# Ordering by hand what a graph kernel does before its first gather

## The chip, the cores and the metric

The program runs on one core of one Trainium2 chip. The metric is the device time of one execution in microseconds (us). A core has five engines with a queue each: TensorE (PE in the profile), VectorE (DVE), ScalarE (ACT), GpSimd (POOL) and SyncE (SP). DMAs are issued from the queues of SP, ACT and POOL.

## What is computed

There are N = 4096 nodes with 128 features in x and a 0/1 matrix adj of 4096 x 4096, in which each row has about 32 ones. Two layers follow one another, both over the neighbours that adj lists:

```
# layer 0, graph attention with 8 heads
Wh  = einsum('nd,hde->hne', x, W)
f1  = einsum('hnd,hd->hn', Wh, a1);  f2 = einsum('hnd,hd->hn', Wh, a2)
e   = leaky_relu(f1[:, :, None] + f2[:, None, :], 0.2)
att = softmax(where(adj > 0, e, -9e15), axis=-1)
h   = elu(einsum('hnm,hmd->hnd', att, Wh))
x1  = layernorm(x + elu(concat_heads(h) @ W1 + b1)) * gamma + beta
# layer 1, quantiles over the neighbours
keep = neighbours, less every m-th one (m = ceil(n/2) where n > 5, else 1)
agg  = mean of the 0.25, 0.5 and 0.75 quantiles of x1 over keep
out  = (0.5*agg + 0.5*x1) @ Wl.T + bl + x1
```

## The kernel before

Since a row has few neighbours, the kernel doesn't multiply by adj. It finds the list of each node's neighbours, sorts the nodes of a block by their number of neighbours, and gathers rows of x from DRAM by list. The 32 tiles of 128 nodes are worked on in three blocks of 4, 9 and 19 tiles (BLOCKS).

**The search** (`neighbours`) turns a tile of adj into lists. ACT takes the sign of half a tile (L568, `sgn`, two buffers). PE makes 512 keys at a time in PSUM (two buffers), each from two matmuls: L607 with `markb` marks a neighbour, and L610 adds its place, from the table `parts` (64 x 4096, zeros but for rows 0 and 32). DVE takes the eight largest keys of each 128 columns (L574, four MAX8), and picks the tile's 64 largest in eight rounds of MAX8 and MATCH_REPLACE8 (L579, L581) into `rec[:, t, 0:64]`, while the keys of the next tile are made. The search is a Python generator. It yields once for each 512 keys; I call that a piece. For the first block of four tiles there are 43 pieces, numbered from 0: 32 with keys, eight in which only the last tile's rounds of picking are left, and three for `complete_records`, which counts, takes out the removed neighbours and writes the lists as integers. Loads of adj (1 MB each, three buffers) go out on ACT's queue, the next one after each sign (L561).

**The rows** (`node_rows`) bring x into `rec`, multiply W by a1 and a2 on DVE (L507, L510) into `wa`, a 128 x 16 matrix, and then for each of the 32 tiles: PE transposes x (L514), ACT copies that to `xT` (L516), PE multiplies it by `wa` (L518), ACT copies the result to `F` (L519); two buffers for each. DVE clamps F into `rec` (L521) and derives a bound check from it (L523 to L528). Four DMAs write rows of 136 numbers (x and f2) to `xt_d` in DRAM, which is what the attention gathers.

**After that**, `rank_by_count` gives each node its place in the block by number of neighbours (DVE and PE; its last operation is L750, `ranks`). POOL scatters the four tiles of `rec` to DRAM by rank (L187), SP reads them back as `R` (L786), DVE makes lists and attention terms of them (L787 to L820, `f1b` and `f1x`), and POOL starts to gather (L178, `G<-xt_d,idx`). From here on POOL gathers to the end: rows of x for the attention (1180 gathers), then rows of x1 for the quantiles (1024).

**What sets the order.** Two parts of the kernel are a `manual_schedule` over DVE, PE, ACT and POOL: in them each of these engines issues its instructions in the order in which the program emits them. These are the attention with the searches of blocks 1 and 2 (from L382), and the sort at the end. Everything ahead of them, so the search of block 0 and the rows, is left to the framework's scheduler, which picks the next instruction for each engine itself. SP's order is always the scheduler's. Where a hand-ordered part's instructions fall among others of the same engine is the scheduler's too. An engine carries out its queue in order.

The tables `own` and `ownT` (L240 to L257) hold, for each width of list, which rows belong to which node; the attention reads them. `before` is a triangular mask for the ranks.

Of the kernel before, what the change touches and what calls it, by code (L numbers as in the profile page):

```python
# [9 lines left out]
F32 = mybir.dt.float32  # L10
BF16 = mybir.dt.bfloat16
I32 = mybir.dt.int32
AF = mybir.ActivationFunctionType
ALU = mybir.AluOpType
# [5 lines left out]
P = 128  # L20
N = 4096
# [180 lines left out]
def kernel(  # L202
# [30 lines left out]
    eps_t = const.tile([P, 1], F32, name="eps_t")  # L233
    nc.vector.memset(eps_t, EPS)
    pidx = const.tile([P, 1], F32, name="pidx")
    iota(nc, pidx, [[0, 1]], cm=1)
    jp1 = const.tile([P, L], F32, name="jp1")
    iota(nc, jp1, [[1, L]], base=1)

    own = {}  # L240
    for w in (32, 16, 8, 4):
        k = P // w
        v = const.tile([P, k], F32, name=f"v{w}")
        iota(nc, v, [[-w, k]], cm=1)
        own[w] = const.tile([P, k], F32, name=f"own{w}")
        nc.vector.tensor_scalar(own[w], v, 0.0, None, ALU.is_ge)
        nc.vector.scalar_tensor_tensor(own[w], v, float(w), own[w], ALU.is_lt, ALU.mult)


    ownT = {}  # L250
    for w in (32, 16, 8, 4):
        k = P // w // 4
        v = const.tile([4, k, P], F32, name=f"vT{w}")
        iota(nc, v, [[-4 * w, k], [1, P]], cm=-w)
        ownT[w] = const.tile([4, k, P], F32, name=f"ownT{w}")
        nc.vector.tensor_scalar(ownT[w], v, 0.0, None, ALU.is_ge)
        nc.vector.scalar_tensor_tensor(ownT[w], v, float(w), ownT[w], ALU.is_lt, ALU.mult)  # L257

    vecs = const.tile([P, 4, D], F32, name="vecs")
    W_sb = const.tile([P, H, D], F32, name="W_sb")  # L260
    W1_sb = const.tile([P, H, D], F32, name="W1_sb")
    nc.sync.dma_start(W_sb, W.rearrange("h d e -> d h e"))
    wa = const.tile([P, 2 * H], F32, name="wa")
    WlT = const.tile([P, D], F32, name="WlT")
    total = const.tile([1, 1], I32, name="total")
    bad = const.tile([P, 5, NT], F32, name="bad")
    consts = dict(
        W_sb=W_sb, W1_sb=W1_sb, vecs=vecs, eps_t=eps_t, ident=ident, own=own, ownT=ownT
    )
    own_i = const.tile([P, NT], I32, name="own_i")  # L270


# [5 lines left out]
    adjp = tc.alloc_tile_pool(name="adjp", bufs=2, side="right")  # L278
    cp = tc.alloc_tile_pool(name="cnt", bufs=2, side="right")
    kp = tc.alloc_tile_pool(name="key_ps", bufs=2, space=PSUM)  # L280
    nc.gpsimd.iota(
        rec.bitcast(I32)[:, :, R_OWN], pattern=[[P, NT]], base=0, channel_multiplier=1
    )
    parts = adjp.tile([64, N], BF16, name="parts", bufs=1)
    markb = adjp.tile([P, P], BF16, name="markb", bufs=1)
    nc.vector.memset(oneb, 1.0)
    nc.vector.tensor_scalar(markb, ident, MARK, None, ALU.mult)

    nc.gpsimd.memset(parts, 0.0)
    iota(nc, parts[0:1, :], [[-64, N // 64], [0, 64]], base=N)  # L290
    iota(nc, parts[32:33, :], [[0, N // 64], [-1, 64]])
    rowi = adjp.tile([P, P], F32, name="rowi", bufs=1)
    iota(nc, rowi, [[1, P]])
    nc.vector.tensor_scalar(before, rowi, pidx, None, ALU.is_gt)

    def search(t0, n):
        return neighbours(
            tc, adjp, cp, kp, rec, num, adj, t0, n, parts, markb, oneb, bad, jp1, pidx
        )

    for _ in search(0, BLOCKS[0]):
        pass
    with tc.tile_pool(name="setup", bufs=1) as sp, tc.tile_pool(
        name="setup_ps", bufs=2, space=PSUM
    ) as pp:
        node_rows(tc, sp, pp, rec, x, W_sb, a1, a2, Wl, wa, WlT, ident, bad, xt_d)
        nc.sync.dma_start(W1_sb, W1.rearrange("(h e) o -> e h o", e=P))
        for i, v in enumerate((b1, gamma, beta, bl)):
            nc.sync.dma_start(vecs[:, i, :], v.partition_broadcast(P))
        for i, big in enumerate((-BIG, BIG)):  # L310
            fill = sp.tile([P, D], F32, name=f"fill{i}")
            nc.vector.memset(fill, big)
            nc.sync.dma_start(x1_d[N + i * P : N + (i + 1) * P, :], fill)
    attp = tc.alloc_tile_pool(name="att", bufs=2, reuse_waits="tile")
    pp = tc.alloc_tile_pool(name="att_ps", bufs=1, space=PSUM)
# [2 lines left out]


    weigh, store, tail = [], [], []  # L320
    consts["small"] = pp.tile([P, 512], F32, name="small")

    narrow = {
# [58 lines left out]
    with tc.manual_schedule(engines=ORDERED):  # L382
        ranks = rank_by_count(tc, cp, kp, num, jp1, before, oneb, 0, BLOCKS[0])
        for v in store_records(0, 0, ranks):
            scatter(nc, *v)
        for b, n in enumerate(BLOCKS):
            last = b == len(BLOCKS) - 1
            if last:
                cp.release()
                adjp.release()  # L390
                keep = tc.alloc_tile_pool(name="keep", bufs=1, side="right")
                wt = keep.tile([P, NT, L], F32, name="wt")
                idx = keep.tile([P, NT, L], I32, name="idx")
                cp = tc.alloc_tile_pool(name="cnt_all", bufs=2, side="right", reuse_waits="tile")
                pieces, left = None, 0
            else:
                pieces, left = search(t0 + n, BLOCKS[b + 1]), pieces_of(BLOCKS[b + 1])
            ready.append(prepare(b, 0, t0))
            for i in range(n):
                among = []  # L400
                if last and 2 < i < n - 5:
                    among = [
                        (all_d, rec[:, t, 0:REC1], ranks[:, t : t + 1])
                        for t in range((i - 3) * NT // (n - 8), (i - 2) * NT // (n - 8))
                    ]
                if not last and i == n - 1:

                    for _ in pieces:
                        pass
                    left = 0  # L410
# [12 lines left out]
                if last and i == n - 5:  # L423
                    R = cp.tile([P, NT, REC1], F32, name="R", bufs=1)
                    nc.sync.dma_start(R, all_d.rearrange("(t p) w -> p t w", p=P))
                    pieces = lists_of_layer_1(
                        tc, cp, kp, R, jp1, pidx, ones, idx, own_i, bad, total, wt
                    )
                    left = -(-LIST_PIECES // 4)
            for _ in pieces or ():  # L430
                pass
            t0 += n
        for _ in range(5):
            step()
        check_bounds(tc, cp, kp, ones, bad, total)
# [49 lines left out]
        general_quantiles(tc, adj, x1_d, x1T_d, out, ident, WlT, vecs[:, 3, :])  # L485


def node_rows(tc, sp, pp, rec, x, W_sb, a1, a2, Wl, wa, WlT, ident, bad, xt_d):

    nc = tc.nc  # L490
    c = NT // 4
    for i in range(4):
        nc.sync.dma_start(
            rec[:, ts(i, c), R_X : R_X + D],
            x[ts(i, c * P), :].rearrange("(t p) d -> p t d", p=P),
        )
    a_b = sp.tile([P, 2, H * D], F32, name="a_b")
    for i, a in enumerate((a1, a2)):
        nc.sync.dma_start(a_b[:, i, :], a.rearrange("h d -> (h d)").partition_broadcast(P))
    wl_sb = sp.tile([P, D], F32, name="wl_sb")  # L500
    nc.scalar.dma_start(wl_sb, Wl)
    wl_ps = pp.tile([P, D], F32, name="xt_ps")
    nc.tensor.transpose(wl_ps, wl_sb, ident)
    nc.scalar.copy(WlT, wl_ps)
    for i in range(2):
        wprod = sp.tile([P, H, D], F32, name="wprod")
        nc.vector.tensor_tensor(  # L507
            wprod, W_sb, a_b[:, i, :].rearrange("p (h d) -> p h d", h=H), ALU.mult
        )
        nc.vector.tensor_reduce(wa[:, ts(i, H)], wprod, AX.X, ALU.add)  # L510
    F = sp.tile([P, NT, 2 * H], F32, name="F")
    for t in range(NT):
        xt_ps = pp.tile([P, P], F32, name="xt_ps")
# [3 lines left out]
        f_ps = pp.tile([P, 2 * H], F32, name="f_ps")  # L517
        nc.tensor.matmul(f_ps, lhsT=xT, rhs=wa, start=True, stop=True)  # L518
        nc.scalar.copy(F[:, t, :], f_ps)  # L519
    for dst, src in ((R_F1, F[:, :, 0:H]), (R_X + D, F[:, :, H:])):  # L520
        nc.vector.tensor_scalar(rec[:, :, dst : dst + H], src, FMAX, -FMAX, ALU.min, ALU.max)  # L521
    sq = sp.tile([P, NT, 2 * H], F32, name="sq")
    nc.vector.tensor_tensor(sq, F, F, ALU.mult)  # L523
    fm = sp.tile([P, NT], F32, name="fm")
# [1 line left out]

    nc.vector.tensor_scalar(fm, fm, FMAX * FMAX, None, ALU.is_le)
    nc.vector.tensor_scalar(bad[:, 3, :], fm, -1.0, 1.0, ALU.mult, ALU.add)  # L528
    for i in range(4):
        nc.sync.dma_start(  # L530
            xt_d[ts(i, c * P), :].rearrange("(t p) w -> p t w", p=P),
            rec[:, ts(i, c), R_X:],
        )
    pad = sp.tile([P, XW], F32, name="pad")
    nc.vector.memset(pad[:, 0:D], 0.0)
    nc.vector.memset(pad[:, D:], PADF)
    nc.sync.dma_start(xt_d[N:, :], pad)


def groups_of(n):  # L540
# [850 lines left out]
```

## Time and profile before

| | us |
|---|---|
| median of three runs | 3857.79 |
| lowest, highest | 3854.88, 3884.28 |
| profiled execution | 3857.37 |
| its span in the trace | 3855.5 |

| engine | busy us in the span | instructions |
|---|---|---|
| POOL | 2807.9 | 2388 |
| DVE | 2671.4 | 6439 |
| PE | 1253.7 | 5433 |
| ACT | 403.4 | 603 |

The stage that the change touches ends with the first gather at 113.86 us. The rest is attention to some 1884 us and quantiles to the end.

How to read the profile: times count from the start of the span. A line of the timeline has its start, its length, engine, line of the program, operation, output<-input, shapes and count; in brackets stands how long the engine had been idle before it and what it waited for ("<-PE key L610": the matmul that wrote key). A line of the waits has who waited, for whom, the sum, how often, and the longest. PEld is PE's load of weights. "issue" is time for which the trace shows no wait. SPq and ACTq are DMA issues in those engines' queues.

### The profile page before, as it was taken

What the parts mean: (1) busy time and instruction counts of PE and PEld (TensorE: products, weight loads), DVE (VectorE), ACT (ScalarE), POOL (GpSimd) and SP (SyncE); (2) the same over time, 40 slices, a digit from 0 to 9 for tenths busy, and PEclk for the clock granted to TensorE, in tenths of its full rate; (3) what the DMA queues carried; (4) which work ended last, traced back from release to release, by engine and by line L of the source; (5) the groups of instructions that cost most, each with busy time, mean ns of one, the idle gap of its engine ahead of it and who ended that gap; (6) DMA issues with size and microseconds to landing.
All of it is one profiled execution on the core that took longest, in us unless ns stands there. A gap on an engine that the chain in (4) does not pass through costs nothing. (4 is left out here: it accounts for less than half of the span.)

```text
span 3855.5 us, 21960 instructions
## 1 busy us (share of the span) xinstructions
PE 1253.7 (33%) x5433; PEld 961.2 (25%) x5433; DVE 2671.4 (69%) x6439; ACT 403.4 (10%) x603; POOL 2807.9 (73%) x2388
## 2 busy tenths in 40 slices
PE   6483867863746444455600000000000000000001
PEld 2143534543635444444500000000000000000000
DVE  8774688782522222257436888669999999998788
ACT  3111223210111101111100000000000000000000
POOL 1657674577777777777478888877788887888882
PEclk9975666655665555555555555555555555555555
DMA  6423444322222222222111111111111111111110
GB/s 213 153 88 106 150 139 132 122 54 65 54 55 53 54 53 54 64 58 55 34 47 38 41 39 34 38 42 41 41 38 28 32 35 44 38 35 38 38 40 16
DMA packets 110281, 241.25 MB, mean 63 GB/s; under 512 B 46976, under 2 KB 63360, under 8 KB 101952
## 3 DMA queue, kind: packets, MB, share of 16 engines
q0 software_dynamic: 76160, 160.24, 15.3%
q10 hardware_dynamic: 9360, 67.18, 5.1%
q1 hardware_dynamic: 24624, 12.34, 1.3%
q8 instruction: 45, 0.74, 0.1%
q14 instruction: 92, 0.75, 0.1%
HBM read 228.44 MB, written 11.15 MB: 62 GB/s over the span
## 5 line engine op out<-in xcount | busy, mean ns | idle before, releaser
L178 POOL DMA_INDIRECT vals<-x_d,idx x1024 | 1415.6, 1382 | 314.4 <-issue 303.8
L178 POOL DMA_INDIRECT G<-xt_d,idx x1180 | 1173.6, 995 | 483.4 <-issue 339.9
L1117 DVE TENSOR_TENSOR work<-work 128x256 f32<-128x256 f32 (+7 forms) x1168 | 921.5, 823 | 0.7
L1137 PE MATMUL st_ps<-dg,goal 128*128 128x128 f32 x286 | 71.9, 429 | 1791.9 <-DVE goal L1117 1704.4
L1117 DVE TENSOR_TENSOR work<-work,work 128x512 f32<-128x512 f32 (+4 forms) x820 | 584.3, 738 | 1.3
L1137 PEld LDWEIGHTS st_ps<-dg,goal 128*128 128x128 f32 x286 | 63.7, 324 | 1798.4 <-issue 1797.5
L926 PE MATMUL y<-wide,G 128*128 128x32 f32 (+3 forms) x2360 | 480.1, 382 | 21.9 <-DVE wide L914 21.9
L926 PEld LDWEIGHTS y<-wide,G 128*128 128x128 f32 x2360 | 460.0, 297 | 45.8 <-DVE wide L914 24.2
L869 DVE TENSOR_TENSOR z<-G,f1x 128x128 f32<-128x128 f32 (+2 forms) x92 | 29.9, 335 | 471.6 <-DMA G<-xt_d,idx 468.5
L1117 DVE TENSOR_TENSOR work<-vals 128x768 f32<-128x768 f32 (+11 forms) x64 | 128.8, 2028 | 267.8 <-DMA vals<-x_d,idx 265.7
L574 DVE MAX8 first<-key 128x8 f32<-128x128 f32 x1024 | 227.5, 282 | 112.5 <-PE key L610 112.5
L607 PE MATMUL key<-sgn,markb 128*128 128x512 bf16 x256 | 142.0, 555 | 160.9 <-DVE first L574 107.5
L883 PE MATMUL small<-z,own 128*4 128x32 f32 (+3 forms) x436 | 50.4, 284 | 368.1 <-ACT z L876 368.1
L1136 ACT ACTIVATE dg<-ident,wt 128x128 f32<-128x128 f32 x143 | 47.5, 394 | 1105.0 <-PE st_ps L1137 1104.6
L568 ACT ACTIVATE sgn<-adj_t 128x2048 bf16<-128x2048 int32 x64 | 122.1, 1907 | 343.0 <-PE key L607 328.2
L898 PE MATMUL rz<-rden,ownT 4*128 4x32 f32 (+3 forms) x436 | 107.1, 419 | 117.9 <-DVE rden L894 96.5
L610 PE MATMUL key<-parts,oneb 64*128 64x512 bf16 x256 | 140.6, 550 | 6.3 <-POOL parts L196 6.3
L956 PE MATMUL small<-W_sb,late 128*128 128x128 f32 x512 | 118.9, 426 | 33.6 <-DVE late L953 33.6
L898 PEld LDWEIGHTS rz<-rden,ownT 4*128 4x128 f32 x436 | 94.5, 310 | 134.0 <-DVE rden L894 68.3
L187 POOL DMA_INDIRECT out_dram<-o,own_i x32 | 67.9, 2123 | 79.9 <-ACT o L1163 56.2
L883 PEld LDWEIGHTS small<-z,own 128*4 128x4 f32 x436 | 27.1, 102 | 385.8 <-ACT z L876 373.3
L956 PEld LDWEIGHTS small<-W_sb,late 128*128 128x128 f32 x512 | 110.2, 327 | 44.9 <-DVE late L953 43.9
(179 smaller groups left out, 1879.3 us busy)
## 6 DMA issues: line engine op xcount, KB each, us to landing
adj_t<-in_adj_dram ACTq DMA_DIRECT2D x64, 1024.0 KB
G<-xt_d,idx POOLq DMA_INDIRECT x1180
vals<-x_d,idx POOLq DMA_INDIRECT x1024
R<-rec_d SPq DMA_DIRECT2D x128, 26.2 KB
xt_d<-rec SPq DMA_DIRECT2D x4, 544.0 KB
rec<-in_x_dram SPq DMA_DIRECT2D x4, 512.0 KB
W_sb<-in_L_gnn_W_dram SPq DMA_DIRECT2D x2, 512.0 KB
a_b<-in_L_gnn_a_dram SPq DMA_DIRECT2D x2, 512.0 KB
```

The costliest lines, as they stand in the source:

```text
L178: nc.gpsimd.indirect_dma_start(out=dst, out_offset=None, in_=rows, in_offset=bass.IndirectOffsetOnAxis(ap=idx, axis=0),)
L187: return nc.gpsimd.indirect_dma_start(out=rows, out_offset=bass.IndirectOffsetOnAxis(ap=idx, axis=0), in_=src, in_offset=None,)
L568: nc.scalar.activation(sgn, adj_t, AF.Sign, accum_out=cnt[:, i : i + 1])
L574: nc.vector.max(first[:, ts(c0 // CW + c, 8)], key[:, ts(c, CW)])
L607: nc.tensor.matmul(key, lhsT=markb, rhs=sgn[:, ts(b, 512)], start=True, stop=False)
L610: nc.tensor.matmul(key, lhsT=oneb[0:64, :], rhs=parts[:, ts(r, 512)], start=False, stop=True)
L883: nc.tensor.matmul(den[0:4, :].rearrange("p (g r h) -> p r g h", r=k // 4, h=H)[:, r], lhsT=own[w][:, ts(r, 4)], rhs=z[:, layer[i] : layer ...
L898: nc.tensor.matmul(rz[:, layer[i] * H : (layer[i] + w) * H], lhsT=ownT[w][:, r, :], rhs=rden.rearrange("p (g r h) -> p r g h", r=k // 4, h ...
L926: nc.tensor.matmul(yf[:, ts(g, c)], lhsT=G[:, col + g - g0, 0:D], rhs=pf[:, ts(g, c)], start=(i == 0 and g % (w // 2) == w // 2 - 1), stop ...
L956: nc.tensor.matmul(o, lhsT=hv[:, h, :], rhs=consts["W1_sb"][:, h, :], start=(h == 0), stop=(h == H - 1))
L1117: nc.vector.tensor_tensor(slots_of(dst, (j, c, s, m), size), slots_of(a, (i, c, s, m), size), slots_of(b, (i + d, c, s, m), size), op,)
L1137: nc.tensor.matmul(st_ps[:, u, :], lhsT=goal[:, (j * k + u) * D : (j * k + u + 1) * D], rhs=dg, start=(j == 0), stop=False,)
```

## The change

The part ahead of the attention becomes a third hand-ordered region, and its steps are emitted in another order:

- The tables for the keys come first: `parts` (cleared by DVE, no longer by POOL), `oneb`, the two iotas of `parts`, `markb`, and then `pidx`, `jp1`, the own numbers and `rowi`. `before` is made behind the search.
- `node_rows` becomes a generator too. After each piece of the search from piece 1 on, it advances by one step. Step by step: load W; load a1, a2, Wl; then x in four loads, three pieces apart; the two products of W; two tiles of x in each of 16 steps; clamps, the writes to `xt_d` and the padding row; the bound check; Wl's transpose.
- The loads of W, a1, a2 and x are issued from ACT instead of SP.
- `own` and `ownT` are made in the attention's region, behind the ranks and scatters of block 0.
- The padding row and two fill tiles are cleared by POOL, no longer by DVE.

```diff
-    own = {}
-    for w in (32, 16, 8, 4):
...
-    nc.sync.dma_start(W_sb, W.rearrange("h d e -> d h e"))
...
-    nc.gpsimd.memset(parts, 0.0)
...
-    for _ in search(0, BLOCKS[0]):
-        pass
     with tc.tile_pool(name="setup", bufs=1) as sp, tc.tile_pool(
         name="setup_ps", bufs=2, space=PSUM
-    ) as pp:
-        node_rows(tc, sp, pp, rec, x, W_sb, a1, a2, Wl, wa, WlT, ident, bad, xt_d)
+    ) as pp, tc.manual_schedule(engines=ORDERED):
+
+        nc.vector.memset(parts, 0.0)
+        nc.vector.memset(oneb, 1.0)
+        iota(nc, parts[0:1, :], [[-64, N // 64], [0, 64]], base=N)
+        iota(nc, parts[32:33, :], [[0, N // 64], [-1, 64]])
+        nc.vector.tensor_scalar(markb, ident, MARK, None, ALU.mult)
+        iota(nc, pidx, [[0, 1]], cm=1)
+        iota(nc, jp1, [[1, L]], base=1)
+        nc.gpsimd.iota(
+            rec.bitcast(I32)[:, :, R_OWN], pattern=[[P, NT]], base=0, channel_multiplier=1
+        )
+        iota(nc, rowi, [[1, P]])
+        rows = node_rows(tc, sp, pp, rec, x, W, W_sb, a1, a2, Wl, wa, WlT, ident, bad, xt_d)
+        for i, _ in enumerate(search(0, BLOCKS[0])):
+            if i > 0:
+                next(rows, None)
+        for _ in rows:
+            pass
+        nc.vector.tensor_scalar(before, rowi, pidx, None, ALU.is_gt)
         nc.sync.dma_start(W1_sb, W1.rearrange("(h e) o -> e h o", e=P))
...
-            nc.vector.memset(fill, big)
+            nc.gpsimd.memset(fill, big)
...
         for v in store_records(0, 0, ranks):
             scatter(nc, *v)
+
+        own = {}
+        for w in (32, 16, 8, 4):
+            k = P // w
+            v = const.tile([P, k], F32, name=f"v{w}")
+            iota(nc, v, [[-w, k]], cm=1)
...
+        ownT = {}
...
@@ node_rows
     nc = tc.nc
     c = NT // 4
+    load = nc.scalar.dma_start
+    load(W_sb, W.rearrange("h d e -> d h e"))
+    yield
+    a_b = sp.tile([P, 2, H * D], F32, name="a_b")
+    for i, a in enumerate((a1, a2)):
+        load(a_b[:, i, :], a.rearrange("h d -> (h d)").partition_broadcast(P))
+    wl_sb = sp.tile([P, D], F32, name="wl_sb")
+    load(wl_sb, Wl)
+    yield
     for i in range(4):
-        nc.sync.dma_start(
+        for _ in range(3):
+            yield
+        load(
             rec[:, ts(i, c), R_X : R_X + D],
             x[ts(i, c * P), :].rearrange("(t p) d -> p t d", p=P),
         )
...
-    wl_ps = pp.tile([P, D], F32, name="xt_ps")
-    nc.tensor.transpose(wl_ps, wl_sb, ident)
-    nc.scalar.copy(WlT, wl_ps)
     for i in range(2):
         wprod = sp.tile([P, H, D], F32, name="wprod")
...
         nc.vector.tensor_reduce(wa[:, ts(i, H)], wprod, AX.X, ALU.add)
+        yield
     F = sp.tile([P, NT, 2 * H], F32, name="F")
     for t in range(NT):
         xt_ps = pp.tile([P, P], F32, name="xt_ps")
         nc.tensor.transpose(xt_ps, rec[:, t, R_X : R_X + D], ident)
         xT = sp.tile([P, P], F32, name="xT", bufs=2)
         nc.scalar.copy(xT, xt_ps)
         f_ps = pp.tile([P, 2 * H], F32, name="f_ps")
         nc.tensor.matmul(f_ps, lhsT=xT, rhs=wa, start=True, stop=True)
         nc.scalar.copy(F[:, t, :], f_ps)
+        if t % 2:
+            yield
     for dst, src in ((R_F1, F[:, :, 0:H]), (R_X + D, F[:, :, H:])):
         nc.vector.tensor_scalar(rec[:, :, dst : dst + H], src, FMAX, -FMAX, ALU.min, ALU.max)
+    for i in range(4):
+        nc.sync.dma_start(
+            xt_d[ts(i, c * P), :].rearrange("(t p) w -> p t w", p=P),
+            rec[:, ts(i, c), R_X:],
+        )
+    pad = sp.tile([P, XW], F32, name="pad")
+    nc.gpsimd.memset(pad[:, 0:D], 0.0)
+    nc.gpsimd.memset(pad[:, D:], PADF)
+    nc.sync.dma_start(xt_d[N:, :], pad)
+    yield
...
+    yield
+    wl_ps = pp.tile([P, D], F32, name="xt_ps")
+    nc.tensor.transpose(wl_ps, wl_sb, ident)
+    nc.scalar.copy(WlT, wl_ps)
```

More of the change, by code (lines that the diff above doesn't have):

```diff
@@ L235 @@
     pidx = const.tile([P, 1], F32, name="pidx")
-    iota(nc, pidx, [[0, 1]], cm=1)
     jp1 = const.tile([P, L], F32, name="jp1")
-    iota(nc, jp1, [[1, L]], base=1)
-    own = {}
-    for w in (32, 16, 8, 4):
[L242 to L257, printed above, removed]
     vecs = const.tile([P, 4, D], F32, name="vecs")
@@ L266 @@
     bad = const.tile([P, 5, NT], F32, name="bad")
-    consts = dict(
-        W_sb=W_sb, W1_sb=W1_sb, vecs=vecs, eps_t=eps_t, ident=ident, own=own, ownT=ownT
-    )
     own_i = const.tile([P, NT], I32, name="own_i")
@@ L280 @@
     kp = tc.alloc_tile_pool(name="key_ps", bufs=2, space=PSUM)
-    nc.gpsimd.iota(
-        rec.bitcast(I32)[:, :, R_OWN], pattern=[[P, NT]], base=0, channel_multiplier=1
-    )
     parts = adjp.tile([64, N], BF16, name="parts", bufs=1)
     markb = adjp.tile([P, P], BF16, name="markb", bufs=1)
-    nc.vector.memset(oneb, 1.0)
-    nc.vector.tensor_scalar(markb, ident, MARK, None, ALU.mult)
-    nc.gpsimd.memset(parts, 0.0)
-    iota(nc, parts[0:1, :], [[-64, N // 64], [0, 64]], base=N)
-    iota(nc, parts[32:33, :], [[0, N // 64], [-1, 64]])
     rowi = adjp.tile([P, P], F32, name="rowi", bufs=1)
-    iota(nc, rowi, [[1, P]])
-    nc.vector.tensor_scalar(before, rowi, pidx, None, ALU.is_gt)
     def search(t0, n):
@@ L320 @@
     weigh, store, tail = [], [], []
+    consts = {}
     consts["small"] = pp.tile([P, 512], F32, name="small")
@@ L385 @@
             scatter(nc, *v)
+        own = {}
[3 more added lines that the diff above has]
+            iota(nc, v, [[-w, k]], cm=1)
+            own[w] = const.tile([P, k], F32, name=f"own{w}")
+            nc.vector.tensor_scalar(own[w], v, 0.0, None, ALU.is_ge)
+            nc.vector.scalar_tensor_tensor(own[w], v, float(w), own[w], ALU.is_lt, ALU.mult)
+        ownT = {}
+        for w in (32, 16, 8, 4):
+            k = P // w // 4
+            v = const.tile([4, k, P], F32, name=f"vT{w}")
+            iota(nc, v, [[-4 * w, k], [1, P]], cm=-w)
+            ownT[w] = const.tile([4, k, P], F32, name=f"ownT{w}")
+            nc.vector.tensor_scalar(ownT[w], v, 0.0, None, ALU.is_ge)
+            nc.vector.scalar_tensor_tensor(ownT[w], v, float(w), ownT[w], ALU.is_lt, ALU.mult)
+        consts.update(
+            W_sb=W_sb, W1_sb=W1_sb, vecs=vecs, eps_t=eps_t, ident=ident, own=own, ownT=ownT
+        )
         for b, n in enumerate(BLOCKS):
@@ L485, with node_rows @@
         general_quantiles(tc, adj, x1_d, x1T_d, out, ident, WlT, vecs[:, 3, :])
-def node_rows(tc, sp, pp, rec, x, W_sb, a1, a2, Wl, wa, WlT, ident, bad, xt_d):
+def node_rows(tc, sp, pp, rec, x, W, W_sb, a1, a2, Wl, wa, WlT, ident, bad, xt_d):
     nc = tc.nc
     c = NT // 4
+    load = nc.scalar.dma_start
[7 more added lines that the diff above has]
+    yield
     for i in range(4):
-        nc.sync.dma_start(
+        for _ in range(3):
+            yield
+        load(
             rec[:, ts(i, c), R_X : R_X + D],
@@ L496, in node_rows @@
         )
[L497 to L501, printed above, removed]
-    wl_ps = pp.tile([P, D], F32, name="xt_ps")
-    nc.tensor.transpose(wl_ps, wl_sb, ident)
-    nc.scalar.copy(WlT, wl_ps)
     for i in range(2):
@@ L519, in node_rows @@
         nc.scalar.copy(F[:, t, :], f_ps)
+        if t % 2:
+            yield
     for dst, src in ((R_F1, F[:, :, 0:H]), (R_X + D, F[:, :, H:])):
         nc.vector.tensor_scalar(rec[:, :, dst : dst + H], src, FMAX, -FMAX, ALU.min, ALU.max)
+    for i in range(4):
+        nc.sync.dma_start(
+            xt_d[ts(i, c * P), :].rearrange("(t p) w -> p t w", p=P),
+            rec[:, ts(i, c), R_X:],
+        )
+    pad = sp.tile([P, XW], F32, name="pad")
[3 more added lines that the diff above has]
+    yield
     sq = sp.tile([P, NT, 2 * H], F32, name="sq")
@@ L528, in node_rows @@
     nc.vector.tensor_scalar(bad[:, 3, :], fm, -1.0, 1.0, ALU.mult, ALU.add)
[L529 to L537, printed above, removed]
+    yield
+    wl_ps = pp.tile([P, D], F32, name="xt_ps")
+    nc.tensor.transpose(wl_ps, wl_sb, ident)
+    nc.scalar.copy(WlT, wl_ps)
 def groups_of(n):
```

## The prediction, made before the result was known

> **What bounds the kernel now.** I began with the busy time by stage. The stage that the change touches runs from the start to the first gather of attention rows, at 113.86 us. Columns: stretch, length, then PE, weight loads, DVE, ACT and POOL busy, granted clock, DMA share, GB/s.
>
> ```profile
> 0.00:113.86 113.86, 59.44 (x168) 25.30 (x168) 81.42 (x315) 32.48 (x86) 19.58 (x28) 1.00 0.57 187
> 113.86:300.00 186.14, 124.36 (x348) 56.52 (x348) 155.84 (x643) 40.54 (x41) 124.97 (x131) 0.83 0.40 124
> ```
>
> POOL, which carries the rest of the kernel with its gathers, does next to nothing here. Whatever moves the first gather moves everything behind it, since no later transfer has a date of its own. The waits around it say what the gather needs:
>
> ```profile
> POOL rec_d L187 <- DVE ranks L750: 73.0, 1, 73.0
> DVE bad L787 <- DMA R<-rec_d: 15.6, 3, 14.4
> POOL G L178 <- DVE f1b L815: 5.7, 1, 5.7
> POOL rec_d L187 <- DMA rec_d<-rec,ranks: 5.3, 3, 1.9
> ```
>
> POOL waits 73 us for the ranks, which end at 98.55; four scatters in a row, a read back and f1b then take 15.3 us. So the question is when the ranks are ready. Next the timeline of DVE and PE:
>
> ```profile
> 15.46 1.01 PE L610 MATMUL key<-parts,oneb 64*128 64x512 bf16 x2 [6.26 <-POOL parts L196]
> 21.13 1.23 DVE L507 TENSOR_TENSOR wprod<-W_sb,a_b 128x1024 f32<-128x1024 f32 x1 [3.12 <-DMA a_b<-in_L_gnn_a_dram]
> 26.11 1.68 DVE L574 MAX8 first<-key 128x8 f32<-128x128 f32 x8
> 34.72 0.89 DVE L574 MAX8 first<-key 128x8 f32<-128x128 f32 x4 [4.52 <-PE key L610]
> ```
>
> Keys exist at 16 us, but DVE stands in front of the W products, which wait for a1 and a2, and starts the search at 26.11. At 34.72 PE had stood for Wl. From 26.11 to 98.55 DVE idles some 13 us and works the rest. The projections of x end (last F copy) at 87.14, well inside that. Last, how one projection passes between PE and ACT:
>
> ```profile
> 82.91 0.61 PE L518 MATMUL f_ps<-wa,xT 128*128 128x16 f32 x2 [0.39 <-ACT xT L516]
> 83.35 0.45 PE L514 MATMUL xt_ps<-ident,rec 128*128 128x128 f32 x1
> ...
> 84.47 0.61 PE L518 MATMUL f_ps<-wa,xT 128*128 128x16 f32 x2
> ...
> 84.92 0.45 PE L514 MATMUL xt_ps<-ident,rec 128*128 128x128 f32 x1
> ...
> 85.47 0.27 ACT L516 COPY xT<-xt_ps 128x128 f32<-128x128 f32 x1 [0.17 <-PE xt_ps L514]
> ...
> 85.79 1.14 PE L518 MATMUL f_ps<-wa,xT 128*128 128x16 f32 x4
> ```
>
> Transpose to copy is 0.55 us (84.92 to 85.47), copy to projection 0.32 (to 85.79), projection to the next transpose 0.44 (82.91 to 83.35): **1.31 us per tile of x if nothing overlaps**. The free scheduler keeps two tiles in flight: two projections come 1.56 us apart (82.91, 84.47), 0.78 per tile.
>
> **What the skill says.** "TensorE: Matmul & The Clock Gate", Step-by-step: what each phase is for: matmuls stay in program order, only weight loads are pulled ahead. The trace agrees where the order is already written by hand: PE stands for rden with key matmuls queued right behind.
>
> ```profile
> 180.32 1.22 PE L898 MATMUL rz<-rden,ownT 4*128 4x256 f32 x2 [9.00 <-DVE rden L894]
> 181.47 0.61 PE L607 MATMUL key<-sgn,markb 128*128 128x512 bf16 x1
> ```
>
> "VectorE: DVE Perf Modes", Zero memsets can be issued as uint32 (trn2): one cycle per element, and zeros in bf16 may go as half as many words. The L705 memset of 64 bf16 runs as 32 uint32 in 0.09 us. "DMA: Bandwidth & Descriptors", Issuing engines are not separate DMA queues: another queue saves only the issuer's time. Here the four x loads held SP for 13.11 us. "Perfetto Trace Analysis", Optimizing Scalar/DVE Operations: DVE in a two-port mode and POOL lock each other out. Agreed: L256 on 4x128 took 5.22 us beside the POOL memset of parts, on 4x1024 later 0.67.
>
> **The change part by part.** Times are from the span's start.
>
> *Key tables first.* DVE clears parts after two small memsets, from 1.0. By the page 2048 words take 2.1 us, as bf16 4.3; I take 2.2. POOL's two iotas (3.85 each) end at 10.9 instead of 15.4; the memset of 3.50 and the tables of the attention are gone from before them. Adj is in time (first sign at 6.13). Key to MAX8 takes 0.64, so the search starts on DVE at **11.6, 14.5 us earlier**. The products no longer stand in front.
>
> *Loads on ACT, between those of adj.* W goes out after piece 1, a1, a2 and Wl after piece 2, x after pieces 6, 9, 12, 15. Queued behind each on ACT is the next sign. An x issue took SP 0.57 to 7.30 us, median 2.55. Pieces 6 to 16 last some 16 us and hold three signs (2.1 each): 10 us of issue fits, so I take 0; if each took 7.3, 19 us would stick out. SP loses these issues and nobody waits there. W1 and the vectors stay on SP, may go out at once (0.8 MB) and put adj off by 2.6 us at the 309 GB/s of the first 10 us; first sign 8.7 then, still under the iotas of parts.
>
> *Search up to wa.* Pieces 1 to 7 run at PE's pair of key matmuls, 1.08 us (MAX8 at 28.23 and 29.31): 7.6. Pieces 8 to 16 run at DVE's pace in the ordered search of block 1 (key matmuls from 130.94 to 143.54, eight pieces in 12.6): 9 x 1.58 = 14.2. The products, 2 x (1.23 + 1.22) = 4.9, and 0.3 of small ops: wa stands at 38.6.
>
> *Projections written into the search, two tiles of x in each of 16 pieces.* In emission order PE does a key pair, transpose, projection, transpose, projection, and stands for ACT's copy each time; the next keys are queued behind, and DVE waits for these. From 38.8: 31 x 1.31 = 40.6, plus 14 key pairs with their lead-in at 1.11 = 15.5. A sign ahead of the first copy costs 0.75 (it ends 2.4 into the piece, the copy would start at 1.65): two own, two more of the next block that the scheduler may put there: 2.5. Last projection at 97.4, its copy ends 0.8 later: **98.2, against 87.14 before**. DVE's 1.6 us per piece hides behind PE's 3.7; that is the step on which all turns.
>
> *Tail on DVE.* The clamps wait for that copy, as they stand behind piece 33. Behind them, in order: clamps 0.5, the six remaining best steps 4.2 (0.81 falling to 0.27 in block 1), squares and bound check 1.75, small ops 0.5, then records and ranks. These took about 9.8 us of DVE where they were woven together, and would take 13.8 one after the other (block 1: 6.8 for three tiles, 7.6 scaled to four; ranks 6.2 by the ordered rows from 299.10, less what nine tiles need more). The second ordered part may still be woven into the first: 11. Sum 17.95: ranks at 116.2 instead of 98.55, **+17.6**. Before, most best steps ran while the projections ended; that cover is gone.
>
> *Wl's transpose, fill and pad* move to the end or to POOL, 1 us in all beside idle time: 0.
>
> *Attention tables after the ranks.* On POOL they stand behind the fourth scatter, 9.3 us after the first, and take 0.41 + 2.03. The last iota ends 11.7 after the first scatter; the two largest L256/L257 pairs may then still be due (0.4 + 0.67 + 0.67 + 1.21): 14.7. The first DVE op on R comes 14.1 after (112.95 - 98.84). So +0.6; 0 if they run beside the iotas, +3 if all of it is late. Early on they cost DVE some 17 us before, hidden by the wait for a1 and a2.
>
> *Behind it.* All moves with the first gather, now near 132. The clock falls from 1.00 to 0.50 between 230 and 240. If it falls at the same time, the work of 18 us runs at half speed on a PE busy 6 to 9 tenths, at most +8; if less dense PE work puts it off, as much the other way. I take 0.
>
> **Sum:** 17.6 + 0.6 = +18.2 on the profiled execution's 3857.4 (span 3855.5 plus 1.9): 3875.6, say **3876**. The runs' median, 3857.8, is 0.4 above it.
>
> **The rivals.** *Not slower: the vector engine stays the bound.* If copies were so quick that PE kept up, ranks would come at 11.6 + 7.6 + 25 x 1.58 + 4.9 + 0.3 + 0.8 + 17.95 = 82.7, 15.9 earlier: 3842, and up to 6 more for the last projections; I say **3845**. For it: 14.5 us of early start are sure. Against: 1.31 us. It decides below some 0.3 us per tile. *The exchange overlaps as before* (0.78): 31 x 0.53 = 16.4 back, **3859**; only if emission order did not bind PE. *Much slower: ACT's issue of x.* If each takes 7.3 us, signs and copies queue behind and 19 us come on top: **3895**; it starts to count when an issue exceeds some 2.5 us, and the median lies there.
>
> **Chances.** Forecast 0.62 (own range 3866 to 3887: clock 8, tail 3, parts 2, tables 2), overlap 0.12, not slower 0.16, much slower 0.10. The range, 3849 to 3892, leaves out most of the third and of the last. One per cent, 39 us, is what a measurement of this kernel can tell from no change; all cases but the last lie within: faster 0.02, same 0.90, slower 0.08.
>
> **What would show it.** First MAX8 near 12; pieces 18 to 31 about 3.7 us apart with PE waiting for xT; last F copy near 98; ranks near 116; first gather near 132; DVE idle on PE keys by some 30 us more. The prediction is wrong if pieces stay near 2 us, if ACT shows issues of 5 us and more, or if the gap at the first gather is made up later.

## The result, and the profile after

The changed kernel takes 3879.28 us (median of 20 runs, 3868.46 to 3893.14) where the kernel before took 3859.46 in the same session (20 runs, 3846.25 to 3884.28). The ratio is 1.0045, with a 95% interval of 1.0032 to 1.0058: slower by about half a per cent. I had taken one per cent for the least that can be told from no change; with 20 runs of each kernel the interval tells half a per cent clearly. The profiled execution took 3878.35 us, its span 3876.6, 21.1 longer than before.

First the stages of the changed kernel: start to the first MAX8, to `wa`, to the last copy of F, to the ranks, to the first gather. The columns are those of the stage view of before (stretch, length, PE, weight loads, DVE, ACT and POOL busy, granted clock, DMA share, GB/s).

```profile
0.00:11.71 11.71, 1.20 (x3) 0.31 (x3) 2.16 (x5) 5.29 (x5) 9.05 (x13) 1.00 0.86 317
11.71:41.16 29.45, 19.21 (x35) 3.56 (x34) 25.14 (x96) 8.27 (x9) 1.27 (x7) 1.00 0.99 324
41.16:100.82 59.66, 43.88 (x124) 22.37 (x124) 26.80 (x115) 21.15 (x71) 0.00 (x0) 1.00 0.25 86
100.82:118.70 17.88, 2.51 (x8) 0.70 (x7) 16.55 (x76) 0.27 (x2) 0.00 (x0) 1.00 0.42 125
118.70:136.01 17.31, 0.46 (x1) 0.00 (x0) 6.77 (x23) 0.00 (x0) 6.38 (x12) 1.00 0.14 39
```

In the third row DVE, which does the search, is busy for 26.80 us of 59.66. In the second the DMA engines are full (0.99 at 324 GB/s); I had not looked at that number before. Next the timeline of PE inside one piece of the third stage, and DVE's wait for the keys of the next:

```profile
44.92 0.61 PE L525 MATMUL f_ps<-wa,xT 128*128 128x16 f32 x2 [0.41 <-ACT xT L523]
45.37 0.45 PE L521 MATMUL xt_ps<-ident,rec 128*128 128x128 f32 x1
46.24 0.61 PE L525 MATMUL f_ps<-wa,xT 128*128 128x16 f32 x2 [0.41 <-ACT xT L523]
46.69 0.59 PE L621 MATMUL key<-sgn,markb 128*128 128x512 bf16 x1
...
47.85 0.89 DVE L588 MAX8 first<-key 128x8 f32<-128x128 f32 x4 [1.85 <-PE key L624]
```

Two projections are 1.32 us apart (44.92, 46.24), each behind a wait for ACT's copy, and the key matmul comes after both. The next key matmul comes at 50.39, 3.70 after this one. The waits up to the first gather say the same in sums (who, for whom, us, times, longest):

```profile
POOL rec_d L187 <- issue: 78.8, 1, 78.8
DVE first L588 <- PE key L624: 41.0, 22, 8.3
PEld f_ps L525 <- ACT xT L523: 24.7, 31, 1.6
DVE own L373 <- POOL v L196: 10.1, 1, 10.1
```

POOL waits 78.8 us before the first scatter (73.0 before). DVE stands 41.0 us for keys where it stood 13.5, as the same view of the kernel before says up to its first gather:

```profile
DVE first L574 <- PE key L610: 13.5, 17, 4.5
```

The 31 waits for xT stand in front of the keys. The wait for `v` (POOL's iota) is new: it belongs to the tables that moved behind the scatters.

All kernels that ran, in order of their first gather; times in us from the span's start, medians of the runs, ratio to the kernel before of the same session with its interval:

| kernel | `wa` | last F | ranks | first gather | median | ratio |
|---|---|---|---|---|---|---|
| e9_both_ends_again | 29.4 | 78.9 | 89.2 | 107.1 | 3852.1 | 0.9979 (0.9965 to 0.9992) |
| e4_free_order | 35.1 | 85.2 | 87.8 | 107.8 | 3853.6 | 0.9982 (0.9969 to 0.9995) |
| e8_both_ends | 29.4 | 80.9 | 91.3 | 109.1 | 4453.1 | 0.9976 (0.9954 to 0.9998) |
| e5_one_tile | 29.4 | 84.6 | 96.5 | 112.7 | 3856.3 | 0.999 (0.998 to 1.0) |
| before | 26.2 | 87.1 | 98.6 | 113.9 | 3859.5 | 1 |
| e1_pairs | 41.9 | 80.4 | 98.3 | 116.0 | 3858.9 | 0.9995 (0.9978 to 1.0011) |
| e6_w1_late | 38.5 | 97.8 | 115.7 | 133.3 | 3869.7 | 1.0026 (1.0012 to 1.0039) |
| e7_iotas_early | 41.6 | 101.2 | 119.1 | 135.4 | 3876.5 | 1.0054 (1.0033 to 1.0075) |
| e3_tables_early | 41.8 | 101.5 | 119.3 | 135.5 | 3876.0 | 1.0046 (1.002 to 1.0072) |
| after | 41.2 | 100.8 | 118.7 | 136.0 | 3879.3 | 1.0045 (1.0032 to 1.0058) |
| e2_loads_sp | 45.2 | 104.5 | 122.4 | 140.1 | 3883.0 | 1.006 (1.0038 to 1.0081) |

(e8_both_ends and e9_both_ends_again are one kernel. In the session of e8_both_ends every execution, those of the kernel before too, took some 600 us longer, so of its row only the ratio compares.)

### The profile page after: what moved, and what is told of

It reads as the page before. It is cut to its first block, busy times and chain, and to the rows that moved or that the text cites. A ratio compares the mean times of both kernels' runs of the same rounds, so it can differ in the third digit from the quotient of the medians.

```text
span 3876.6 us, 21960 instructions
## 1 busy us (share of the span) xinstructions
PE 1250.2 (32%) x5433; PEld 949.0 (24%) x5433; DVE 2666.4 (69%) x6436; ACT 405.9 (10%) x603; POOL 2805.6 (72%) x2391
## 5 line engine op out<-in xcount | busy, mean ns | idle before, releaser
L940 PE MATMUL y<-wide,G 128*128 128x32 f32 (+3 forms) x2360 | 467.3, 375 | 28.7 <-DVE wide L928 28.7
L940 PEld LDWEIGHTS y<-wide,G 128*128 128x128 f32 x2360 | 446.2, 289 | 53.4 <-DVE wide L928 31.2
## 6 DMA issues: line engine op xcount, KB each, us to landing
R<-rec_d SPq DMA_DIRECT2D x128, 26.2 KB
```

Of the source, the lines that this page charges most:

```text
L940: nc.tensor.matmul(yf[:, ts(g, c)], lhsT=G[:, col + g - g0, 0:D], rhs=pf[:, ts(g, c)], start=(i == 0 and g % (w // 2) == w // 2 - 1), stop ...
```

## The experiments

Every experiment is the changed kernel with the edit shown, but for e8_both_ends, whose edit is shown against e5_one_tile. My theory was that PE's queue, now in emission order, stands for ACT's copy in each tile with the keys behind it; the rivals put the loss on ACT's loads, on the late tables, or on the moves as a whole.

**e1_pairs: the same steps, but no projection waits for a copy just begun.**

```diff
+    held = []
+    def project():
+        for u, xT in held:
+            f_ps = pp.tile([P, 2 * H], F32, name="f_ps")
+            nc.tensor.matmul(f_ps, lhsT=xT, rhs=wa, start=True, stop=True)
+            nc.scalar.copy(F[:, u, :], f_ps)
+        held.clear()
     for t in range(NT):
+        if t % 2 == 0:
+            project()
...
-        f_ps = pp.tile([P, 2 * H], F32, name="f_ps")
-        nc.tensor.matmul(f_ps, lhsT=xT, rhs=wa, start=True, stop=True)
-        nc.scalar.copy(F[:, t, :], f_ps)
+        held.append((t, xT))
...
+    project()
```

> Changed kernel, but each step projects the two tiles that the step before transposed, and then transposes two more; nothing else. Theory (PE stands for ACT's copy in every projection): PE needs 1.1 + 0.9 + 0.55 = 2.5 us per piece instead of 3.7, so the last F copy comes near 83 instead of 100.8, the first gather near 118 instead of 136, and the time is near 3860, that of the kernel before. Rival (the loads on ACT's queue, or the tables and the tail behind the search, are what costs): pieces may shorten, but the first gather stays above 130 and the time above 3872.

Measured: last F at 80.4, first gather at 116.0, 3858.9 us. PE's timeline in one piece:

```profile
43.84 1.03 PE L524 MATMUL f_ps<-wa,xT 128*128 128x16 f32 x4
44.71 0.67 PE L532 MATMUL xt_ps<-ident,rec 128*128 128x128 f32 x2
45.17 0.63 PE L631 MATMUL key<-sgn,markb 128*128 128x512 bf16 x1
45.74 0.60 PE L634 MATMUL key<-parts,oneb 64*128 64x512 bf16 x1
```

No wait is left; the next key matmul is at 47.60, 2.43 after this one (3.70 before the edit). The number of matmuls and copies is the same. This one edit takes 20 us off the first gather and 20 off the median. **Standing for the exchange between PE and ACT is 20 of the 22 us by which the change put off the first gather; this is shown.**

**e4_free_order: all moves of the change, but the first part isn't ordered by hand.**

```diff
-    ) as pp, tc.manual_schedule(engines=ORDERED):
+    ) as pp:
```

> Changed kernel with the hand-ordered region around the part ahead of the attention taken away; the emission order, the loads on ACT and the late tables stay. Theory (emission order kept PE from having two tiles in flight): the scheduler overlaps the projections again, 0.8 us per tile where nothing else is between, and the first gather comes between 105 and 120, the time between 3848 and 3863. Rival (what costs is the order of loads and tables, which stays): first gather above 130.

Measured: first gather at 107.8, 3853.6 us, faster than the kernel before. PE's timeline:

```profile
60.35 0.61 PE L525 MATMUL f_ps<-wa,xT 128*128 128x16 f32 x2
60.79 0.45 PE L521 MATMUL xt_ps<-ident,rec 128*128 128x128 f32 x1
61.04 0.45 PE L525 MATMUL f_ps<-wa,xT 128*128 128x16 f32 x2
61.33 0.45 PE L521 MATMUL xt_ps<-ident,rec 128*128 128x128 f32 x1
61.57 0.63 PE L621 MATMUL key<-sgn,markb 128*128 128x512 bf16 x1
```

The scheduler puts projections of two earlier transposes close together and doesn't stand either. So the moves of tables and loads together gain 6 us at the first gather, and the emission order lost 28 against the scheduler's (136.0 less 107.8). The exchange is 20 of these. The table shows where the rest can lie: in e1_pairs `wa` is done at 41.9 (35.1 in e4_free_order), and the ranks come 17.9 us after the last copy of F, here only 2.6, since the scheduler doesn't keep the last rounds of the search behind that copy.

**e2_loads_sp: the loads of W, a1, a2 and x from SP.**

```diff
-    load = nc.scalar.dma_start
+    load = nc.sync.dma_start
```

> Changed kernel with the loads of W, a1, a2, Wl and x issued from SP's queue again, so at the start. Theory: pieces with projections stay 3.7 us long; the 2.6 us for which PE stood for a late sign at 22.6 go, so wa stands near 38.6 and the first gather comes near 133.5, the time near 3877. Against it, 4 MB now stand beside the first loads of adj and may put the start off by some us. Rival (ACT's issues cost the time): first gather below 125, time below 3868.

Measured: not what I expected. The first gather comes at 140.1, 4 us later than with the loads on ACT. SP's queue and PE:

```profile
3.04 14.92 SPq L507 DMA_DIRECT2D rec<-in_x_dram  x4
...
18.66 0.58 PE L621 MATMUL key<-sgn,markb 128*128 128x512 bf16 x1 [3.75 <-ACT sgn L582]
26.59 0.58 PE L621 MATMUL key<-sgn,markb 128*128 128x512 bf16 x1 [3.57 <-ACT sgn L582]
```

SP isn't ordered by hand, so it asks for W, a1 and a2 from 0.76 and for all of x from 3.04 us on. They then take their share of the DMA engines while the search wants adj, and the keys stand for two late signs instead of one. The issue of x on ACT, which made my fourth case, is the better place: in the changed kernel the four issues took 0.45, 0.95 and 4.07 us (the last two together).

**e3_tables_early: `own` and `ownT` at the start again.** The two loops move, unchanged, from behind the scatters to ahead of `vecs`.

> Changed kernel with own and ownT made at the start again, as before the change. Theory: the 2 us that the way from the ranks to the first gather took longer go (17.3 to 15.3), but the large ownT operations now stand ahead of the search and wait for POOL's iotas, so the search starts near 14.5 instead of 11.7; first gather near 137, time near 3880. Rival (late tables cost the time): first gather near 126 or less.

Measured: the search starts at 15.06 instead of 11.71, yet `wa` is done at 41.8, only 0.6 later than in the changed kernel, and the first gather comes 0.5 earlier. The stages of e3_tables_early up to the first MAX8, and to `wa`:

```profile
0.00:15.06 15.06, 2.25 (x4) 0.41 (x4) 13.84 (x22) 5.29 (x5) 11.79 (x24) 1.00 0.81 282
15.06:41.78 26.72, 18.29 (x33) 3.46 (x33) 24.89 (x97) 8.28 (x9) 0.83 (x3) 1.00 1.01 335
```

3.35 us of delay nearly vanish. In both kernels the third sign comes at the same time (20.31 here, 20.53 in the changed kernel): the earlier start only made PE stand 3.31 us for it, and here it doesn't stand. What held that sign is the next experiment.

**e6_w1_late: W1 and the four vectors are loaded last.** They stand last in the hand-ordered part in the changed kernel too, but on SP, which issues them from 0.76 us on.

```diff
-        nc.sync.dma_start(W1_sb, W1.rearrange("(h e) o -> e h o", e=P))
+        nc.scalar.dma_start(W1_sb, W1.rearrange("(h e) o -> e h o", e=P))
         for i, v in enumerate((b1, gamma, beta, bl)):
-            nc.sync.dma_start(vecs[:, i, :], v.partition_broadcast(P))
+            nc.scalar.dma_start(vecs[:, i, :], v.partition_broadcast(P))
```

> The changed kernel with one edit: W1 and the four vectors are loaded by ScalarE at the end of the hand-ordered part, not by SyncE at its start. Theory (ScalarE's issue of the fifth load of adj and the sign behind it were late, at 16.20 and 20.53 us, because these 1.5 MB stood in the same queues): the sign moves up to about 18 us, wa is done at 38 to 39 us instead of 41.2, the first gather at about 133.5 instead of 136.0, time some 3876 us. Rival (ScalarE waits for its own loads of adj, W and the a's, which are still there): wa stays at 40.5 to 41.5, the first gather at 135 to 136.5, time 3878 to 3880.

(The expectation says 1.5 MB; the five loads are 512 and four times 64 KB, 0.8 MB.) First the changed kernel, ACT and PE, where the sign came late:

```profile
16.20 0.33 ACTq L575 DMA_DIRECT2D adj_t<-in_adj_dram  x1
17.39 0.39 ACTq L496 DMA_DIRECT2D W_sb<-in_L_gnn_W_dram  x1
17.81 1.97 ACTq L500 DMA_DIRECT2D a_b<-in_L_gnn_a_dram  x2
19.82 0.67 ACTq L502 DMA_DIRECT2D wl_sb<-in_L_gnn_W_dram  x1
20.53 1.91 ACT L582 ACTIVATE sgn<-adj_t 128x2048 bf16<-128x2048 int32 x1 [9.57 <-issue]
...
22.58 0.58 PE L621 MATMUL key<-sgn,markb 128*128 128x512 bf16 x1 [3.31 <-ACT sgn L582]
```

The sign begins 0.04 us behind the end of ACT's last issue, and the trace shows no other wait ("issue"). So it was late because it stood in ACT's queue behind these loads, and the first of them had not gone out until 16.20. Then ACT and DVE of e6_w1_late:

```profile
10.29 0.34 ACTq L575 DMA_DIRECT2D adj_t<-in_adj_dram  x1
...
14.06 0.56 ACTq L502 DMA_DIRECT2D wl_sb<-in_L_gnn_W_dram  x1
14.67 1.91 ACT L582 ACTIVATE sgn<-adj_t 128x2048 bf16<-128x2048 int32 x1 [4.41 <-PE key L621]
...
37.27 1.22 DVE L516 TENSOR_REDUCE wa<-wprod 128x8 f32<-128x1024 f32 x1
```

ACT now issues the fifth load of adj right behind the second sign, all its issues are done 5.9 us earlier, the sign follows them, and PE doesn't stand for it. `wa` is done at 38.5 and the first gather at 133.3, as the theory had it. So 0.8 MB that nobody waits for cost 2.7 us. By the ratios (1.0045 and 1.0026) the time falls by 7 us, more than the gather's 2.8, but both intervals are some 5 us wide to either side, so a surplus isn't shown (see the last section).

**e7_iotas_early: the eight iotas of `own` and `ownT` ahead of the scatters; DVE's half of the tables stays behind the ranks.**

```diff
         iota(nc, rowi, [[1, P]])
+        for w in (32, 16, 8, 4):
+            vs[w] = const.tile([P, P // w], F32, name=f"v{w}")
+            iota(nc, vs[w], [[-w, P // w]], cm=1)
...
-            v = const.tile([P, k], F32, name=f"v{w}")
-            iota(nc, v, [[-w, k]], cm=1)
+            v = vs[w]
```

> The changed kernel with one edit: the eight iotas behind own and ownT are given to GpSimd ahead of the scatters, after the other tables, and only VectorE's part of the tables stays after the ranks. Theory (the way from ranks to the first gather is 2.0 us longer than in the kernel before because VectorE has to wait for the iotas behind the scatters): ranks at 118.7 as in the changed kernel, first gather 15.3 to 16 us after them, at 134 to 134.7 instead of 136.0, time some 3877 us. Rival (the way is longer for another reason: SyncE's reads of the records, or the scatters themselves): the gather still comes 17 us or more after the ranks, at 136, time 3878 to 3880.

In the changed kernel, on DVE and POOL, the tables hold the first look at R (L801):

```profile
128.83 0.17 DVE L373 TENSOR_SCALAR own<-v 128x4 f32<-128x4 f32 x1 [10.13 <-POOL v L196]
...
133.77 1.21 DVE L384 SCALAR_TENSOR_TENSOR ownT<-vT,ownT 4x1024 f32<-4x1024 f32 x1
134.91 0.13 DVE L801 TENSOR_SCALAR bad<-R 128x1 f32<-128x1 f32 x1
136.01 0.97 POOL L178 DMA_INDIRECT G<-xt_d,idx  x1 [4.98 <-issue]
```

In e7_iotas_early they don't:

```profile
134.32 0.15 DVE L806 TENSOR_SCALAR bad<-R 128x1 f32<-128x1 f32 x1 [9.79 <-DMA R<-rec_d]
...
135.44 0.97 POOL L178 DMA_INDIRECT G<-xt_d,idx  x1 [6.04 <-issue]
```

DVE waits for R itself again. From the end of the ranks to the first gather it is now 16.35 us, against 17.31 in the changed kernel and 15.31 before, so both expectations missed by a little: about half of the 2.0 us was the tables. e3_tables_early agrees: with no table behind the ranks its way is 16.15 us, and not the 15.3 that I had expected there. Of the rest, 0.6 lies between ranks and first scatter: 0.88 us in the changed kernel, in e3_tables_early, in e4_free_order and here, 0.29 in the kernel before. What fills it the trace doesn't say.

**e5_one_tile: a better hand order.** One tile per step, projected a step after its transpose; loads of x and the products come earlier; W1 and the vectors last (as e6_w1_late), the iotas early (as e7_iotas_early), `before` ahead of the search.

```diff
-        for _ in range(3):
-            yield
+        yield
         load(
...
     for t in range(NT):
+        project()
...
+        held.append((t, xT))
-        if t % 2:
+        if t < 22 or t % 2:
             yield
+    project()
```

> The hand-ordered part of the changed kernel with the projections spread and skewed: every step projects the tile transposed in the step before and transposes one more (two more in the last steps, where there is no key to make), the loads of x and the two products come earlier, W1 and the vectors are loaded last from ScalarE, the mask before and the iotas of own and ownT come ahead of the scatters. Theory (what cost time was the exchange of TensorE and ScalarE inside a step, and the late products): a step then costs what VectorE needs, 0.82 for four MAX8 and 0.95 for one round of the best, about 1.8 us; wa by 31 us, the last copy of F by 83, ranks by 87, the first gather by 103, and with 3741 us behind it and 2 outside the profile about 3846 us, below both kernels. Rival (the exchange is only one of several limits: signs and loads share ScalarE's queue, and TensorE has 1.13 us of keys and 0.6 us per tile in each step): steps of 2.2 us or more, first gather after 108 us, time 3852 or more, no better than the free order.

Measured: steps of 1.79 us, all rounds of the search but the last done at 75.1, but the first gather only at 112.7. ACT's and DVE's timelines of e5_one_tile show why:

```profile
72.62 0.17 ACT L531 COPY F<-f_ps 128x16 f32<-128x16 f32 x1 [0.70 <-PE f_ps L530]
72.97 0.27 ACT L539 COPY xT<-xt_ps 128x128 f32<-128x128 f32 x1 [0.17 <-PE xt_ps L537]
73.93 0.17 ACT L531 COPY F<-f_ps 128x16 f32<-128x16 f32 x1 [0.70 <-PE f_ps L530]
...
84.64 0.50 DVE L545 TENSOR_SCALAR rec<-F 128x256 f32<-128x256 f32 x2 [9.56 <-ACT F L531]
```

While a key pair lies between a transpose and its projection, PE waits for nothing. When the keys are done, the same order is a bare exchange of 1.31 us a tile (72.62 to 73.93), and DVE stands 9.56 us for the last copy, because the clamps stand in its queue ahead of the last round of the search. So the steps came as the theory said, and the first gather and the time fell on the rival's side, for a reason that neither had named. By its interval this kernel isn't told from the kernel before.

**e8_both_ends and e9_both_ends_again: two tiles per step where there are no keys, and the clamps two steps later.**

```diff
     for t in range(NT):
-        project()
+        if t <= 21 or t % 2:
+            project()
...
-        if t < 22 or t % 2:
+        if t < 21 or t % 2 == 0:
             yield
     project()
+    for _ in range(2):
+        yield
```

> e5_one_tile with its last stage mended: where the keys are done, two tiles are projected in a step instead of one by one (1.31 us each in e5_one_tile, where VectorE stood 9.56 us for the last F), and the clamps come two steps later. Theory (the exchange, where no key lies between its halves, costs 1.31 us a tile wherever it stands): two tiles then take about 1.3 us together, the last copy of F is at 76 to 78 us, ranks at 85 to 88, the first gather 16.4 us after them at 102 to 105; with 3741 us behind and 2 outside the profile about 3847 us, below the kernel before by some 12. Rival (the time doesn't follow the first gather one to one any more, since e5_one_tile's gather came 1.2 us earlier than in the kernel before, its median 3.5 us): ranks and gather as said, time 3842 or less, or 3852 and more.

Where e8_both_ends ran, the kernel before took 4462.55 us too, against 3860 everywhere else, so only the ratio counts: 0.9976 (0.9954 to 0.9998). The last copy of F (80.9), the ranks (91.3) and the first gather (109.1) all came later than expected. The same kernel once more:

> The kernel of e8_both_ends once more, since all kernels took some 600 us longer where that ran, with idle time ahead of instructions on every engine that no engine's work explains, and its first gather came at 109.1 us, the last copy of F at 80.7. Theory: with the usual 3860 us of the kernel before, pairs of tiles take 1.74 us as there (the order on TensorE, not the place, sets it), the last copy of F at 79 to 81, ranks at 90 to 91, the first gather 16.4 us after them at 106 to 108, time 3849 to 3853, ratio 0.997 to 0.9985. Rival: what disturbed the engines in that run also stretched the first 110 us, the gather comes at 102 to 105 as first expected, time 3844 to 3849.

Measured: 3852.1 us, ratio 0.9979 (0.9965 to 0.9992), first gather at 107.1, as the theory says. DVE's and ACT's lines of e9_both_ends_again:

```profile
71.72 0.17 ACT L531 COPY F<-f_ps 128x16 f32<-128x16 f32 x1 [0.49 <-PE f_ps L530]
...
73.46 0.17 ACT L531 COPY F<-f_ps 128x16 f32<-128x16 f32 x1 [0.49 <-PE f_ps L530]
...
78.89 0.50 DVE L548 TENSOR_SCALAR rec<-F 128x256 f32<-128x256 f32 x2 [4.71 <-ACT F L531]
```

Two tiles take 1.74 us, 0.87 a tile: better than 1.31, not the 0.65 of my first expectation, since the copies of a pair still stand between its transposes and its projections. DVE still waits 4.71 us. From the ranks to the first gather it takes 17.8 us, not the 16.4 of the expectation: VectorE's small operations for `own` stand among the last ones on the records, and these end 0.8 us after the ranks. The kernel is faster than both: by 8 us than the kernel before, and by some 26 than the changed one by the ratios (0.9979 against 1.0045). Against the scheduler's free order with the same moves (e4_free_order, 0.9982) the intervals show no gain.

## Why the prediction was right

The prediction was 3876.0 us; measured were 3879.3 as a median and 3878.35 in the profiled execution. Step by step:

- **Start of the search**: predicted 11.6, measured 11.71. The clearing of `parts` took 1.76 us for 2048 words, less than the 2.2 that I took and than the 2.1 estimated from the Trainium skill ("VectorE: DVE Perf Modes", Zero memsets can be issued as uint32 (trn2): one cycle per element); the iotas set the start, as assumed.
- **`wa`**: predicted 38.6, measured 41.2. The terms that were mis-sized are "W1 and the vectors ... still under the iotas of parts" and the 0 for the loads on ACT. The first sign did come under the iotas (5.96), but with these bytes queued early ACT's issues of adj, W, a1, a2 and Wl went out late, and the third sign, behind them in ACT's queue, kept PE standing for 3.31 us. e6_w1_late shows that the bytes were the cause: without them `wa` is done at 38.5. That the loss, 2.7, is near the 2.6 us that I had priced for the transfer may be chance, since it came about in another way.
- **Projections**: predicted 59.6 us, measured 59.66 (41.16 to 100.82). Pieces without a sign took 3.70 to 3.71, predicted 2 x 1.31 + 1.11 = 3.73. e1_pairs shows that the exchange is the cause.
- **Tail**: predicted 17.95, measured 17.88. The clamps did stand in front of the best steps that were left. That the sum is right to a tenth is luck: the best steps took 4.7 us (predicted 4.2), the small operations, records and ranks 10.9 (predicted 11.5).
- **Tables behind the ranks**: predicted 0.6, measured 2.0, inside the bound of 3. About 1 of it is the tables (e7_iotas_early, e3_tables_early), 0.6 the later first scatter.
- **Behind the first gather**: predicted 0; the rest of the span is 3740.6 us, against 3741.6. The clock fell to 0.50 with the work, between 250 and 260 us instead of between 230 and 240.

The sum is 18.2 + 2.6 + 1.4 = 22.2 at the first gather (136.01 less 113.86), less 1.0 behind it: 21.1 in the profile. The medians differ by 19.8.

Of the rivals, "the exchange overlaps as before" needed emission order not to bind PE; it does, and e4_free_order, where it doesn't bind, ends even below. "The vector engine stays the bound" didn't happen here, but e5_one_tile and e9_both_ends_again show that its condition can be met: 1.79 us per step with PE waiting for nothing. Its 3845 still wasn't reached, because of the last tiles (4.7 us of standing in e9_both_ends_again) and a way from the ranks to the first gather that is 2.5 us longer than before. "Much slower: ACT's issue of x" fell with 0.45, 0.95 and 4.07 us for the four issues; it was the issues ahead of x, from 16.20 to 20.49 us, that cost time. The Trainium skill's point that another queue saves only the issuer's time ("DMA: Bandwidth & Descriptors", Issuing engines are not separate DMA queues) held, yet I drew too little from it: both queues fill the same DMA engines, and here a load on SP's queue held up issues on ACT's (the fifth of adj went out at 16.20 with W1 queued, at 10.29 without).

## What to carry to other kernels

When code is put under a hand-written order, look for every round trip between two engines inside one step (transpose, copy, matmul): nothing will overlap it any more but what is written between its halves, so put a step's worth of other work there, also in the last steps, where that other work has run out. A load that is "last" in the program is not last on a queue whose order is not kept: here 0.8 MB that went out early, while the DMA share was near 1, cost 2.7 us. On an engine that both issues loads and computes, look at what stands behind an issue, too, since a late issue makes that late. A wait of an engine is hidden only up to the next point at which the same resource is short; ask for the whole stretch, not for the first use.

## What the runs showed that I had not expected

- The DMA engines were nearly full for the first 41 us of the changed kernel (share 0.86, then 0.99, at 317 and 324 GB/s). "DMA: Bandwidth & Descriptors", Queues, rings and completion order, says that each DMA engine serves the queues in turn, packet by packet. No run here shows the turns; e2_loads_sp, where early loads on SP made the signs on ACT late, and e6_w1_late fit them.
- ACT's issue itself was held up: the fifth load of adj went out at 16.20 us though the sign before it had ended at 10.97, and at 10.29 in e6_w1_late. In e2_loads_sp, too, both late signs follow within 0.1 us on an issue of adj that went out late (at 16.21 and 24.11). That ACT waited for room in the full queues is an inference; the trace names no releaser.
- The part behind the first gather looks less rigid in the profiles than it is. Span less first gather was 3739.7 to 3743.5 us in before, after, e1_pairs, e3_tables_early, e5_one_tile, e7_iotas_early and e9_both_ends_again, but 3736.4 in e6_w1_late, 3734.9 in e4_free_order and 3730.6 in e2_loads_sp. Each is one execution, and those of one kernel differ by up to 38 us (3846 to 3884 in the kernel before); the profiled ones of e4_free_order and e2_loads_sp were among the fastest of theirs. With the median in place of the profile's span, median less first gather is 3740.5 to 3745.9 us in all kernels of the usual sessions but e6_w1_late (3736.4, with some 5 us of uncertainty). So the time follows the first gather one to one as far as these runs can tell.
- In the session of e8_both_ends all executions took some 600 us longer at the same granted clock (0.578) and with the same busy times (POOL 2791 us, against 2800 in e5_one_tile). The time lies in idle stretches; what caused them stays open.
